# LoRA adapters gated once for both batches, with A and B taken through DRAM

## The chip, the cores and the metric

The kernel runs on one core of one Trainium2 chip. The core has TensorE (PE) for matrix products, VectorE (DVE), ScalarE (ACT) and GpSimd (POOL) for elementwise work, SyncE (SP) as an issuer of DMAs, an on-chip memory of 128 partitions (SBUF), and PSUM, into which TensorE writes. The metric is the device time of one execution in microseconds. The time before is the median of three runs.

## What is computed

x is (2, 1024, 2048), ctx is (2, 2048, 2048), the FFN kernel is 2048 x 2048, all f32. Cut to what matters here:

```python
x = x + matmul(fake_quant(layernorm(x)), fake_quant(ctx))        # cross attention part
z = layernorm(x)
base_out = matmul(z, kernel) + bias                              # FFN
x_flat = z.reshape(8, -1, 2048)                                  # 8 groups of 256 tokens
A_eff = einsum('bn,nri->bri', gate, lora_A)                      # 8 x 32 x 2048, from 16 adapters
B_eff = einsum('bn,nor->bor', gate, lora_B)                      # 8 x 2048 x 32
Ax    = einsum('bri,bti->btr', A_eff, x_flat)
delta = einsum('bor,btr->bto', B_eff, Ax)
Ax_s  = einsum('ri,bti->btr', lora_A_shared, x_flat)             # the shared adapter
delta = delta + einsum('or,btr->bto', lora_B_shared, Ax_s)
out   = x + base_out + delta
```

"Gating" is the making of A_eff and B_eff: a weighted sum over 16 adapters, with one set of 16 weights for each of 8 groups of tokens. Groups 0 to 3 belong to the first batch, 4 to 7 to the second.

## The kernel before

**Tiling.** The two batches are worked through one after the other by the loop at line 672. A batch has 1024 tokens, held in y as four tiles of 256 tokens (g = 0 to 3) by 2048. The 2048 output columns are four blocks of 512 (n = 0 to 3).

**Stages of a batch.** First, x is normalised, quantised and transposed into c1T (prep_x), and the context is quantised one block n at a time into c2[n] (quantise: a loaded slice goes through ScalarE into a q2b buffer, and from there through DVE into bf16). column_term sums a block over the rows on TensorE (tile pc). xattn_pair multiplies (tile pa) one group g by one block n, in two halves j of 16 matmuls; a ScalarE instruction writes the start value of each half into PSUM beforehand (line 340), and DVE adds the result to y and takes statistics. Then y is normalised into z, transposed on TensorE (tile ptz) and copied by ScalarE into the tiles zq, which are also stored to DRAM as zs. lora_ax multiplies z by the gated and shared A (tiles px, axT). Last comes the FFN as seven outer products of seven inner ones (product, line 590; chains fu, fv, fw), with the operands loaded as blocks and combined on DVE and GpSimd. Delta adds the adapters' output in between (tile pl); it reads B from DRAM into bp by a DMA that ScalarE issues (line 454). While the first batch is at its last outer product, the second batch's first context block and x are prepared (meanwhile).

**Gating.** The adapters' A and B lie in DRAM with 512 rows, one for each adapter and rank, in four chunks c of 8 ranks x 16 adapters = 128 rows. A matmul with the matrix gmat (128 rows by 4 groups x 8 ranks = 32 columns) gives one chunk's gated rows. In gated (line 357) the four chunks of one column block write four strips of 32 partitions of one PSUM tile:

```python
row = (2 * h + c) * GP
nc.tensor.matmul(ps[row : row + GP, :], gmat..., t[:, c, :], start=True, stop=True, skip_group_check=True)
```

DVE copies that tile into a q2b buffer (line 376). lora_a_step transposes the four 128-column pieces on TensorE (tile pga) and lets DVE put them into acat, the left operand of lora_ax (line 387). lora_b_step writes the q2b buffer with eight DMAs on SP into the batch's own DRAM tensor bd[b] (line 397). Both are called four times in each batch: A for n = 0, 1 between the quantise steps of block 2 (line 717), A for n = 2, 3 after groups 1 and 2 of block 2 (line 730), B for n = 0 after block 2 (line 733) and for n = 1 to 3 after the groups of block 3 (line 751). gmat is made anew at the top of each batch (line 673).

**What sets the order.** Each engine works through its own list in order. The lists are made at build time by a scheduler that orders instructions by a model of their times, so an instruction can stand between others that come earlier or later in the text; DVE's sums in the FFN are tied in a fixed line. Loads of context and adapters are issued by load_next in the order of the list todo (lines 155 to 165), into the ten buffers lit; SP issues them, the weight loads (line 520), the writes to bd and, in the FFN, the reads of zs. q2b has three buffers, shared by quantise and gated. The PSUM pool ps_m has two buffers, shared by the tiles pt, pc, pg, pga, ptz and px. The pools hand out buffers in turn.

Of the kernel before, what the change touches and what calls it, by code (L numbers as in the profile page):

```python
# [20 lines left out]
P = 128  # L21
# [45 lines left out]
def tile_quant_xattn_then_lora_ffn(  # L67
# [30 lines left out]
    H = D // 2  # L98
    KH = KT // 2
    KQ = KT // 4  # L100
    GP = GPB * RC

    const = ctx.enter_context(tc.tile_pool(name="const", bufs=1))
    small = ctx.enter_context(tc.tile_pool(name="small", bufs=4))
# [15 lines left out]
    bp = Bufs([const.tile([P, NB], F32, tag=f"bp{i}", name=f"bp{i}") for i in range(2)])  # L120
    bias_b = Bufs([const.tile([P, NB], F32, tag=f"bias{i}", name=f"bias{i}") for i in range(1)])
    axT = const.tile([P, GPB // 2, GT], F32, tag="axT", name="axT")
    gmat = const.tile([P, 2, GPB // 2, RC], F32, tag="gmat", name="gmat")
    st1 = const.tile([P, MT, NN, 6], F32, tag="st1", name="st1")
    st2 = const.tile([P, MT, NN, 6], F32, tag="st2", name="st2")
    r_s = const.tile([P, MT], F32, tag="r_s", name="r_s")
# [4 lines left out]
    ]  # L131


    bd = [dram.tile([GPB, 2, R, D], F32, tag=f"bd{b}", name=f"bd{b}") for b in range(B)]

    def bf(t, n):

# [18 lines left out]
    for b in range(B):  # L156
        for n in range(2):
            todo.extend((b, raw_src(b, n, r)) for r in range(KT // 2))
        for n in range(2, 4):
            for r in range(KT // 2):  # L160
                todo.append((b, raw_src(b, n, r)))
                if r in ((3, 7) if n == 2 else (5, 7)):
                    todo.extend((b, ad_src(la, 2 * (n - 2) + r // 6 if n == 3 else r // 4, h)) for h in range(2))
        for n in range(NN):
            todo.extend((b, ad_src(lb, n, h)) for h in range(2))
    loaded = deque()
    ahead = [2]
# [14 lines left out]
    def next_loaded():  # L182
        return loaded.popleft()
# [55 lines left out]
    )  # L239
    gval = const.tile([P, GB], F32, tag="gval", name="gval")  # L240
    nc.vector.tensor_tensor(gate_b, gate_b, m_ad.unsqueeze(1).to_broadcast([P, GB, NL]), ALU.mult)
    for b in range(B):
        for i in range(2):
            nc.vector.tensor_reduce(
                gval[:, ds(b * GPB + i * 2, 2)], gate_b[:, b * GPB + i : (b + 1) * GPB : 2, :], AX.X, ALU.add
            )

    def norm_stats(stats, name):  # L250
# [103 lines left out]
        return summed  # L354


    def gated(nm):

        ps = ps_m.tile([P, NB], F32, tag="pm", name=f"pg_{nm}")
        for h in range(2):  # L360
            buf, t = next_loaded()
            for c in range(2):
                row = (2 * h + c) * GP
                nc.tensor.matmul(  # L364
                    ps[row : row + GP, :],
                    gmat.rearrange("p i a r -> p (i a r)"),
                    t[:, c, :],
                    start=True,
                    stop=True,
                    skip_group_check=True,  # L370
                )
            lit.give(buf)
            load_next()
        st = q2b.take()
        sf = st.rearrange("p k n -> p (k n)").bitcast(F32)
        nc.vector.tensor_copy(sf, ps)
        return st, sf

    def lora_a_step(b, n):

        st, sf = gated(f"a{b}_{n}")
        pt = ps_m.tile([P, KQ, P], F32, tag="pm", name=f"pga_{b}_{n}")
        for k in range(KQ):
            nc.tensor.transpose(pt[:, k, :], sf[:, ds(k * P, P)], ident)
        q2b.give(st)
        for g in range(GPB):
            nc.vector.tensor_copy(
                acat[:, ds(n * KQ, KQ), own_col[g], :].rearrange("p k (c r) -> p k c r", c=NC),
                pt.rearrange("p k (c i a r) -> p i a k c r", c=NC, i=2, r=RC)[:, g % 2, g // 2],
            )  # L390

    def lora_b_step(b, n):

        st, sf = gated(f"b{b}_{n}")
        for c in range(NC):
            for i in range(2):
                nc.sync.dma_start(
                    out=bd[b][i::2, i, ds(c * RC, RC), ds(n * NB, NB)],
                    in_=sf[ds(c * GP + i * (GP // 2), GP // 2), :],
                )  # L400
        q2b.give(st)

    def prep_z(b, m, zq, wk):

# [34 lines left out]
    class Delta:  # L439
# [7 lines left out]
        def step(self):  # L447
            if not self.units:
                return
            pr, n, j = self.units.popleft()  # L450
            cols = ds(n * NB, NB)
            if j == 0:
                self.bp, self.bb = bp.take(), bias_b.take()
                nc.scalar.dma_start(
                    out=self.bp, in_=bd[self.b][ds(2 * pr, 2), :, :, cols].rearrange("g s r n -> (g s r) n")
                )
# [213 lines left out]
            big.give(t)  # L670

    for b in range(B):
        nc.vector.tensor_tensor(
            gmat.rearrange("p i a r -> p (i a) r"),
            m_rk.unsqueeze(1).to_broadcast([P, GPB, RC]),
            gval[:, ds(b * GPB, GPB)].unsqueeze(2).to_broadcast([P, GPB, RC]),
            ALU.mult,
        )
        if b == 0:
            open_c2(0)  # L680
            prep_x(0, 0, c1T, wk)
# [21 lines left out]
        for g in range(2, GPB):  # L703
            for m in range(g * MG, (g + 1) * MG):
                with tc.issue_after(opened.ins):
                    prep_x(b, m, c1T, wk)
            for n in range(2):
                xattn_pair(b, n, g, c1T, c2[n])
                if g + 1 == GPB:
                    close_c2(n)  # L710
                    open_c2(n + 2)
                    bp.give(colt.pop(n))
                    if n == 0:
                        for r in range(NR):
                            quantise(c2[2], r)
                            if r % 4 == 3:
                                lora_a_step(b, r // 4)
                        column_term(b, 2, c2[2])
        if b == 0:
            for pr in range(GPB // 2):  # L720
                nc.sync.dma_start(out=acat[:, :, 3 * pr + 1, :], in_=a_sh)
            for bb in range(B):
                for g in range(GPB):
                    nc.sync.dma_start(out=bd[bb][g, 1 - g % 2], in_=b_sh)
        for g in range(GPB):
            xattn_pair(b, 2, g, c1T, c2[2])
            for r in {0: range(3), 1: range(3, 6), 2: range(6, 8), 3: ()}[g]:
                quantise(c2[3], r)
            if 1 <= g <= 2:
                lora_a_step(b, g + 1)  # L730
            if g == 2:
                column_term(b, 3, c2[3])
        lora_b_step(b, 0)
        close_c2(2)
        bp.give(colt.pop(2))
        first = Operands(b, 0)
# [2 lines left out]
        for g in range(GPB):  # L739
            xattn_pair(b, 3, g, c1T, c2[3])  # L740
            big.give(c1T_bufs[g])
            if g == 0:
                first.block("b11")
                first.load("b12")
            elif g == 1:
                first.block("b12")
                first.comb("t1", "b12", "b11", ALU.subtract)
            elif g == 2:
                first.load("b22")
            if g < 3:  # L750
                lora_b_step(b, g + 1)
            if g > 0:
                zqs[g - 1] = [lit.take() for _ in range(4)]
                group_z(b, g - 1, wk, zqs[g - 1])
            if g == 2:

                lora_ax(b, 0, [zqs[0], zqs[1]])
                for i in range(2):
                    for j in range(2):
                        first.t[f"a{i + 1}{j + 1}"] = zqs[i][j]  # L760
                        lit.give(zqs[i][2 + j])
# [127 lines left out]
```

## Time and profile before

Median of three runs: 1131.94 us (1130.91 to 1132.06).

| What | Value |
|---|---|
| the profiled execution's own time | 1128.31 us |
| its span | 1126.5 us |
| granted TensorE clock | 1.00 |
| q2b<-lit on ScalarE (quantise, line 310) | 64 of 1230 ns |
| pg_a, pg_b on TensorE (line 364) | 64 + 64 records, mean 605 ns |
| pga on TensorE (line 384) | 32 records, mean 274 ns |
| adapter loads on SP (line 179) | 32 + 32 of 256 KB |
| bd<-q2b on SP (line 397) | 64 of 32 KB |
| HBM read, written | 224.99 MB, 37.75 MB |

Times count from the start of the span. "Busy" is time in which an engine executes, "idle before" is the time just before an instruction in which its engine did nothing, with what released it. A matmul of f32 operands makes two records in the profile, one of bf16 operands makes one; successive matmuls overlap, so the start of the next instruction tells more than a record's own duration. By the chain of work that ended last, TensorE carries 81% of the span, DVE 8%, DMA 6% and ScalarE 4%. The first batch's gating runs from 102.9 us (first pg_a) to 189.6 us, the second's from 644.1 to 731.1 us. The FFN of the first batch is in full course from about 242 us, that of the second from about 782 us.

### The profile page before, as it was taken

How to read it: one execution, taken by the hardware profiler on the slowest of the kernel's cores; microseconds unless marked ns; L12 is line 12 of the kernel's file. 1: busy time of each engine (PE TensorE's matmuls, PEld its weight loads, DVE VectorE, ACT ScalarE, POOL GpSimd, SP SyncE). 2: the span in 40 equal slices, each digit the busy share in tenths (PEclk: the TensorE clock that was granted, in tenths of full speed). 3: DMA queues.
4: the chain of work that ended last, by engine and by line, in shares of the span. 5: the costliest groups of instructions: out<-in, count | busy, mean ns of one | idle time of the engine just before them, and what ended most of it. 6: DMA issues, size and time to landing. Idle time of an engine off the chain costs nothing.

```text
span 1126.5 us, 10325 instructions
## 1 busy us (share of the span) xinstructions
PE 1076.9 (96%) x3782; PEld 483.3 (43%) x3782; DVE 734.3 (65%) x961; ACT 261.4 (23%) x342; POOL 263.9 (23%) x105
## 2 busy tenths in 40 slices
PE   1689999999999999999999999999999999999998
PEld 0344435544444444444444444455444444444443
DVE  4675538566595767568766654666668586865861
ACT  4975413210001010001384761232000000000000
POOL 0000000234344422525000000022435343243600
PEclk9999999999999999999999999999999999999999
DMA  8991936886689747489866093688668875649611
GB/s 304 395 245 38 294 109 239 306 304 211 247 281 373 265 172 261 158 304 338 302 204 188 1 268 96 235 328 313 233 219 289 298 254 183 253 146 321 213 38 56
DMA packets 120771, 261.33 MB, mean 232 GB/s; under 512 B 11920, under 2 KB 16144, under 8 KB 119568
## 3 DMA queue, kind: packets, MB, share of 16 engines
q1 hardware_dynamic: 99264, 218.65, 57.0%
q10 hardware_dynamic: 21456, 42.02, 10.8%
q8 instruction: 30, 0.49, 0.2%
q14 instruction: 21, 0.17, 0.0%
HBM read 224.99 MB, written 37.75 MB: 233 GB/s over the span
## 4 chain that ended last, share of the span: by engine, by line
PE 81%; DVE 8%; DMA 6%; ACT 4%; issue 1%; SPq 0%; DVEq 0%; ACTq 0%
PE fu L590 33%; PE fv L590 17%; PE pa L342 13%; PE fw L590 8%; PE pl L462 3%; DVE st L279 2%; PE ptz L413 2%; DMA y<-in_x_dram 2%; PE pc L327 2%; DVE big L539 1%; DMA zs<-lit 1%; DMA bd<-q2b 1%; PE pg_a L364 1%; ACT big L291 1%; PE pg_b L364 1%
## 5 line engine op out<-in xcount | busy, mean ns | idle before, releaser
L590 PE MATMUL fu<-big,lit 128*128 128x512 f32 x896 | 396.3, 594 | 0.6 <-DVE y L608 0.6
L539 POOL TENSOR_TENSOR lit<-lit,lit 128x1024 f32<-128x1024 f32 x56 | 161.9, 2898 | 539.5 <-DMA zs<-lit 207.6
L590 PEld LDWEIGHTS fu<-big,lit 128*128 128x128 f32 x896 | 167.7, 190 | 212.4 <-issue 211.4
L342 PE MATMUL pa<-big,big 128*128 128x512 bf16 x1024 | 234.1, 379 | 8.4 <-ACT pa L340 7.2
L590 PE MATMUL fv<-big,lit 128*128 128x512 f32 x448 | 198.1, 594 | 0.0
L530 POOL TENSOR_TENSOR lit<-lit,lit 128x1024 f32<-128x1024 f32 x40 | 101.6, 2539 | 285.6 <-DMA lit<-zs 253.5
L539 DVE TENSOR_TENSOR big<-big,big 128x2048 f32<-128x2048 f32 x56 | 158.9, 2840 | 5.9 <-PE ptz L413 5.3
L608 DVE TENSOR_TENSOR y<-y,fu 128x1024 f32<-128x1024 f32 (+1 forms) x98 | 113.5, 1193 | 69.5 <-PE fu L590 69.2
L342 PEld LDWEIGHTS <-big 128*128 128x128 bf16 x1024 | 97.5, 98 | 139.1 <-issue 31.9
L590 PEld LDWEIGHTS fv<-big,lit 128*128 128x128 f32 x448 | 84.3, 190 | 108.4 <-issue 108.4
L608 DVE TENSOR_TENSOR y<-y,fv 128x1024 f32<-128x1024 f32 x48 | 56.8, 1218 | 92.5 <-PE fv L590 92.5
L459 ACT COPY pl<-bias 128x1024 f32<-128x1024 f32 x32 | 32.6, 1018 | 346.4 <-DVE y L472 320.9
L310 ACT ACTIVATE q2b<-lit,sc,inv 128x1024 int16<-128x1024 f32 x64 | 76.5, 1230 | 139.6 <-DMA lit<-in_ctx_dram 128.1
L530 DVE TENSOR_TENSOR big<-big,big 128x2048 f32<-128x2048 f32 x40 | 100.7, 2517 | 5.1 <-DMA big<-in_w_dram 5.1
L590 PE MATMUL fw<-big,lit 128*128 128x512 f32 x224 | 100.6, 596 | 0.0
L351 DVE SCALAR_TENSOR_TENSOR y<-pa,k_s,y 128x1024 f32<-128x1024 f32 x32 | 41.0, 1282 | 85.6 <-PE pa L342 85.5
L340 ACT ACTIVATE pa<-bp,r_s 128x512 f32<-128x512 f32 x64 | 42.9, 683 | 98.4 <-DVE y L351 35.4
L590 PEld LDWEIGHTS fw<-big,lit 128*128 128x128 f32 x224 | 41.3, 190 | 52.0 <-issue 50.5
L608 DVE TENSOR_TENSOR y<-y,fw 128x1024 f32<-128x1024 f32 x24 | 28.4, 1215 | 52.7 <-PE fw L590 52.7
L299 PE MATMUL pt<-ident_h,big 128*128 128x128 bf16 x256 | 20.5, 231 | 29.9 <-ACT big L294 29.7
L279 DVE BATCH_NORM_STATS2 st<-y 128x6 f32<-128x512 f32 x64 | 41.7, 675 | 2.7 <-DMA y<-in_x_dram 2.7
L472 DVE TENSOR_TENSOR y<-pl,y 128x512 f32<-128x512 f32 x64 | 41.0, 681 | 1.2
(75 smaller groups left out, 591.2 us busy)
## 6 DMA issues: line engine op xcount, KB each, us to landing
big<-in_w_dram SPq DMA_DIRECT2D x96, 1024.0 KB
lit<-zs SPq DMA_DIRECT2D x88, 512.0 KB
lit<-in_ctx_dram SPq DMA_DIRECT2D x64, 512.0 KB
out_dram<-y ACTq DMA_DIRECT2D x30, 512.0 KB
zs<-lit ACTq DMA_DIRECT2D x24, 512.0 KB
y<-in_x_dram SPq DMA_DIRECT2D x8, 1024.0 KB
lit<-in_lora_a_dram SPq DMA_DIRECT2D x32, 256.0 KB
lit<-in_lora_bt_dram SPq DMA_DIRECT2D x32, 256.0 KB
```

Source lines behind the costliest of these rows:

```text
L279: nc.vector.bn_stats(st1[:, m, n, :], ym[:, ds(n * NB, NB)])
L310: nc.scalar.activation(qi, t, AF.Relu, bias=z2, scale=inv2)
L340: nc.scalar.activation(pa[:, j, :], colt[n], AF.Identity, bias=r_s[:, m : m + 1])
L342: nc.tensor.matmul(pa[:, j, :], c1T[g][:, k, ds(j * P, P)], c2[k // 8][:, k % 8, :], start=False, stop=(k == KT - 1), skip_group_check=True,)
L351: summed = nc.vector.scalar_tensor_tensor(yp, pa, s12, yp, ALU.mult, ALU.add)
L459: nc.scalar.copy(pl, self.bb.unsqueeze(1).to_broadcast([P, 2, NB]))
L462: nc.tensor.matmul(pl[:, i, :], axT[rows, pr, ds(j * P, P)], self.bp[rows, :], start=False, stop=True, skip_group_check=True,)
L472: line(nc.vector.tensor_add(yb, pl[:, i, :], yb))
L530: line(eng.tensor_tensor(got[0], got[0], got[1], ALU.add if terms[1][2] > 0 else ALU.subtract))
L539: line(eng.tensor_tensor(out_t, at[p], at[q], op))
L590: nc.tensor.matmul(ps[:, m, :], at[:, k, ds(m * P, P)], bt[:, k, :], start=(opens and k == 0), stop=(ends and k == KQ - 1), skip_group_che ...
L608: line(nc.vector.tensor_tensor(yp, yp, chains[chain][:, js, :], ALU.add if sign > 0 else ALU.subtract))
```

## The change

gmat gets 64 columns: all eight groups of both batches, made once before the loop. gated is called for one half h (two chunks) at a time: two matmuls that write two strips of 64 partitions, one copy into q2b, and four DMAs on SP into a DRAM tensor. It is called only in the first batch, eight times for A (tensor ad) and eight for B (tensor bd, now one for both batches). A no longer goes from q2b to the transposes: in each batch lora_at_step reads two column blocks of the batch's half of ad back into a lit buffer, twice, and makes the eight transposes and four wider copies into acat. These reads stand after group 1 of block 2 and after group 0 of block 3. The adapter loads of the second batch are taken out of todo.

```diff
-    GP = GPB * RC
+    GP = GB * RC
-    bd = [dram.tile([GPB, 2, R, D], F32, tag=f"bd{b}", name=f"bd{b}") for b in range(B)]
+    ad = dram.tile([2, GB // 2, R, D], F32, tag="ad", name="ad")
+    bd = dram.tile([GB, 2, R, D], F32, tag="bd", name="bd")
...
-                if r in ((3, 7) if n == 2 else (5, 7)):
+                if b == 0 and r in ((3, 7) if n == 2 else (5, 7)):
...
-        for n in range(NN):
+        for n in range(NN if b == 0 else 0):
             todo.extend((b, ad_src(lb, n, h)) for h in range(2))
...
-    def gated(nm):
+    def gated(nm, n, h, dst):
         ps = ps_m.tile([P, NB], F32, tag="pm", name=f"pg_{nm}")
-        for h in range(2):
-            buf, t = next_loaded()
-            for c in range(2):
-                row = (2 * h + c) * GP
-                nc.tensor.matmul(ps[row : row + GP, :], ...)
-            lit.give(buf)
-            load_next()
+        buf, t = next_loaded()
+        for c in range(2):
+            nc.tensor.matmul(ps[c * GP : (c + 1) * GP, :], ...)
+        lit.give(buf)
+        load_next()
         st = q2b.take()
         sf = st.rearrange("p k n -> p (k n)").bitcast(F32)
         nc.vector.tensor_copy(sf, ps)
-        return st, sf
+        for c in range(2):
+            for i in range(2):
+                nc.sync.dma_start(
+                    out=dst[i][:, ds((2 * h + c) * RC, RC), ds(n * NB, NB)],
+                    in_=sf[ds(c * GP + i * (GP // 2), GP // 2), :],
+                )
+        q2b.give(st)
...
+    def lora_a_step(n):
+        for h in range(2):
+            gated(f"a_{n}_{h}", n, h, ad)
+    def lora_b_step(n):
+        own = [bd[i::2, i] for i in range(2)]
+        for h in range(2):
+            gated(f"b_{n}_{h}", n, h, own)
+    def lora_at_step(b, n2):
+        buf = lit.take()
+        t = flat(buf)
+        nc.sync.dma_start(
+            out=t, in_=ad[:, ds(b * GPB // 2, GPB // 2), :, ds(2 * n2 * NB, 2 * NB)].rearrange("i a r n -> i (a r) n")
+        )
+        for n in range(2):
+            pt = ps_m.tile([P, KQ, P], F32, tag="pm", name=f"pga_{b}_{n2}_{n}")
+            for k in range(KQ):
+                nc.tensor.transpose(pt[:, k, :], t[:, ds((n * KQ + k) * P, P)], ident)
+            for pr in range(GPB // 2):
+                nc.vector.tensor_copy(
+                    acat[:, ds((2 * n2 + n) * KQ, KQ), 3 * pr : 3 * pr + 3 : 2, :],
+                    pt.rearrange("p k (i a r) -> p a k i r", i=2, r=R)[:, pr],
+                )
+        lit.give(buf)
...
-                            if r % 4 == 3:
-                                lora_a_step(b, r // 4)
+                            if b == 0 and r % 4 == 3:
+                                lora_a_step(r // 4)
...
-            if 1 <= g <= 2:
-                lora_a_step(b, g + 1)
+            if b == 0 and 1 <= g <= 2:
+                lora_a_step(g + 1)
+            if g == 1:
+                lora_at_step(b, 0)
...
-        lora_b_step(b, 0)
+        if b == 0:
+            lora_b_step(0)
...
-            if g < 3:
-                lora_b_step(b, g + 1)
+            if g == 0:
+                lora_at_step(b, 1)
+            if b == 0 and g < 3:
+                lora_b_step(g + 1)
```

More of the change, by code (lines that the diff above doesn't have):

```diff
@@ L122, in tile_quant_xattn_then_lora_ffn @@
     axT = const.tile([P, GPB // 2, GT], F32, tag="axT", name="axT")
-    gmat = const.tile([P, 2, GPB // 2, RC], F32, tag="gmat", name="gmat")
+    gmat = const.tile([P, 2, GB // 2, RC], F32, tag="gmat", name="gmat")
     st1 = const.tile([P, MT, NN, 6], F32, tag="st1", name="st1")
@@ L241, in tile_quant_xattn_then_lora_ffn @@
     nc.vector.tensor_tensor(gate_b, gate_b, m_ad.unsqueeze(1).to_broadcast([P, GB, NL]), ALU.mult)
[L242 to L246, printed above, removed]
+    for i in range(2):
+        nc.vector.tensor_reduce(gval[:, ds(i * GB // 2, GB // 2)], gate_b[:, i::2, :], AX.X, ALU.add)
+    nc.vector.tensor_tensor(
+        gmat.rearrange("p i a r -> p (i a) r"),
+        m_rk.unsqueeze(1).to_broadcast([P, GB, RC]),
+        gval.unsqueeze(2).to_broadcast([P, GB, RC]),
+        ALU.mult,
+    )
     def norm_stats(stats, name):
@@ L354, in xattn_pair @@
         return summed
-    def gated(nm):
+    def gated(nm, n, h, dst):
         ps = ps_m.tile([P, NB], F32, tag="pm", name=f"pg_{nm}")
-        for h in range(2):
-            buf, t = next_loaded()
-            for c in range(2):
-                row = (2 * h + c) * GP
[L364 to L371, printed above, removed]
-            lit.give(buf)
-            load_next()
+        buf, t = next_loaded()
+        for c in range(2):
+            nc.tensor.matmul(
+                ps[c * GP : (c + 1) * GP, :],
+                gmat.rearrange("p i a r -> p (i a r)"),
+                t[:, c, :],
+                start=True,
+                stop=True,
+                skip_group_check=True,
+            )
+        lit.give(buf)
+        load_next()
         st = q2b.take()
@@ L376, in gated @@
         nc.vector.tensor_copy(sf, ps)
-        return st, sf
[L379 to L395, printed above, removed]
+        for c in range(2):
             for i in range(2):
                 nc.sync.dma_start(
-                    out=bd[b][i::2, i, ds(c * RC, RC), ds(n * NB, NB)],
+                    out=dst[i][:, ds((2 * h + c) * RC, RC), ds(n * NB, NB)],
                     in_=sf[ds(c * GP + i * (GP // 2), GP // 2), :],
@@ L401, in lora_b_step @@
         q2b.give(st)
+    def lora_a_step(n):
[19 more added lines that the diff above has]
+                    pt.rearrange("p k (i a r) -> p a k i r", i=2, r=R)[:, pr],
+                )
+        lit.give(buf)
     def prep_z(b, m, zq, wk):
@@ L454, in step @@
                 nc.scalar.dma_start(
-                    out=self.bp, in_=bd[self.b][ds(2 * pr, 2), :, :, cols].rearrange("g s r n -> (g s r) n")
+                    out=self.bp, in_=bd[ds(self.b * GPB + 2 * pr, 2), :, :, cols].rearrange("g s r n -> (g s r) n")
                 )
@@ L672, in tile_quant_xattn_then_lora_ffn @@
     for b in range(B):
[L673 to L678, printed above, removed]
         if b == 0:
@@ L721, in tile_quant_xattn_then_lora_ffn @@
                 nc.sync.dma_start(out=acat[:, :, 3 * pr + 1, :], in_=a_sh)
-            for bb in range(B):
-                for g in range(GPB):
-                    nc.sync.dma_start(out=bd[bb][g, 1 - g % 2], in_=b_sh)
+            for g in range(GB):
+                nc.sync.dma_start(out=bd[g, 1 - g % 2], in_=b_sh)
         for g in range(GPB):
```

## The prediction

> **What bounds the kernel now.** I read the engine totals first, then the slices, then TensorE's waits, then its timeline where the adapters are gated.
>
> ```profile
> PE 1076.9 (96%) x3782; PEld 483.3 (43%) x3782; DVE 734.3 (65%) x961; ACT 261.4 (23%) x342; POOL 263.9 (23%) x105
> ```
>
> ```profile
> PE   1689999999999999999999999999999999999998
> ```
>
> The first line is the engine totals, the second TensorE's busy tenths in 40 slices. TensorE (PE) is busy for 96% of 1126.5 us, and the idle part lies in the first three slices. From about 90 us on only TensorE's own work, or a new wait of it, can move the end. Its waits say the same of the two stretches that the change touches, 95 to 245 us in the first batch and 560 to 785 us in the second: the longest single wait there is 1.1 us.
>
> How gating looks on TensorE (columns: start, duration, instruction, tiles, records):
>
> ```profile
> 132.27 1.05 PE L364 MATMUL pg_a<-lit,gmat 128*32 128x512 f32 x2
> 133.25 3.63 PE L342 MATMUL pa<-big,big 128*128 128x512 bf16 x16
> 136.80 1.06 PE L364 MATMUL pg_a<-lit,gmat 128*32 128x512 f32 x6
> 137.79 2.33 PE L342 MATMUL pa<-big,big 128*128 128x512 bf16 x10
> ...
> 188.61 1.07 PE L364 MATMUL pg_b<-lit,gmat 128*32 128x512 f32 x8
> 189.61 2.98 PE L342 MATMUL pa<-big,big 128*128 128x512 bf16 x13
> ```
>
> One f32 matmul makes two records. The reader is to see that one matmul (x2), three (x6) and four (x8) take the same time from start to the next line: 0.98, 0.99, 1.00 us. The four write different 32-column strips and run at once; a group costs about 0.98 us whatever its size. So what counts is groups. Of the 16 calls of gated, 10 are split by the scheduler (x2, then x6 later) and 6 are whole: 26 groups, 13 in each batch, 12.8 us per batch.
>
> **Second batch: what goes.** All 13 groups go: 12.8 us. The 0.4 us that pga waited there for DVE's copy goes too. The 16 transposes stay (lora_at_step makes the same number), so they change nothing. The loads removed (32 of 256 KB, 8.4 MB) and 32 writes to bd lay beside TensorE's work and are worth nothing themselves; they free SP's queue ahead of the context loads and the weight loads. What is late next? The column sum pc_2 needs eight quantised slices at 1.23 us of ScalarE each, 9.8 us after the first column block's buffer comes free, and TensorE now has some 3 us less to do in that time; I give back 0.6 us. The two reads of ad stand before the weight loads on SP, long after ad was written. Second batch: -13.2 + 0.6 = **-12.6 us**.
>
> **First batch: TensorE's own work.** A 64-column tile leaves room for two matmuls at once. The nearest row is lora_ax, whose pairs of 64-column tiles do run so (its group, with busy us, mean ns and idle before it; then its piece in the chain of work that ended last, with start and us):
>
> ```profile
> L429 PE MATMUL px<-lit,acat 128*64 128x256 f32 x192 | 28.5, 381 | 0.0
> ```
>
> ```profile
> 741.73 7.06 PE px L429 x64
> ```
>
> These are 32 matmuls in 7.06 us, so 16 pairs at 0.44 us for 256 columns; for 512 columns 0.86 us, and about 0.98 with the change of tiling. In the built programs' order the first batch issues, for A: 1 matmul, later 1+2; 2; 2; 1, later 1+2; 2+2; for B: 2+2; 2+2+2; 2; 2+2. A lone group is 0.98 us, each further step behind it 0.86 (in "1+2" the first runs beside one of the two). A: 2.82 + 1.96 + 2.82 + 1.84; B: 1.84 + 2.70 + 0.98 + 1.84; sum 16.8 us against 12.8 now: **+4.0 us**.
>
> Here a rule speaks against the change. The Trainium skill, TensorEngine Tiling (Array Packing), Theoretical Speedup, gives up to 4x for 32 columns and up to 2x for 64. By it the 16 calls need 16 packs of four before and 8 x 2 packs of two after: no TensorE time saved. By the row it is 26 groups before and 16.8 us after, because the scheduler had cut 10 packs in two. The same page (Key Properties) says that a change of tiling mode drains TensorE; the row's 0.98 against 0.86 puts that at 0.12 us. I take the rows: 25.6 - 16.8 = 8.8 us of TensorE work saved in all.
>
> **First batch: new waits.** Each half now goes PSUM, DVE copy, q2b, four writes on SP, DRAM. The rows (two groups as before, then one tile's writes with least, median and longest issue in ns):
>
> ```profile
> L376 DVE COPY q2b<-pg_a 128x512 f32<-128x512 f32 x8 | 5.4, 681 | 0.0
> L387 DVE COPY acat<-pga 128x128 f32<-128x128 f32 x32 | 7.1, 283 | 5.0 <-PE pga L384 5.0
> ```
>
> ```profile
> L397 SPq DMA_DIRECT2D bd<-q2b x64: 567/567/831, 156.7 to 741.2; - x64
> ```
>
> SP issues four writes in 2.3 us; then they must land. No row shows an ad write. The chain of waits has two bd writes:
>
> ```profile
> 187.25 8.71 DMA zs<-lit
> 195.98 5.46 DMA bd<-q2b
> 201.46 7.32 DMA bd<-q2b
> ```
>
> 5.5 and 7.3 us, but behind two weight loads and zs stores. The low end is the about 2 us of the Trainium skill's DMA: Bandwidth & Descriptors (the fixed cost, mostly the wait for the write's receipt). Ahead of the first ad writes only two context loads (1 MB) stand in the queue, so I take 3 us and keep 7.3 for the range. A q2b buffer is then away 0.7 + 2.3 + 3 = 6 us, and there are three for quantise and gating.
>
> I laid the new order against the old clock (DVE, ScalarE and SP each in order):
> - Behind the first two q2b copies on DVE stand two statistics (1.3 us), and behind them the quantise steps; ScalarE quantises with one q2b buffer until the ad writes land. The start value of pa_1_3's second half is queued behind that on ScalarE, at 115.7 us; TensorE wants it at 114.8: 0.9 us. Slices 7 and 8 of pc_2 get their buffers when ad lands, about 115 and 117.5 us; pc_2 reads them near 121: nothing, with 3 us of cover.
> - pc_2 now stands behind most of pa_1_3, so pa_2_0 waits for pc_2's DVE and ScalarE steps: 0.5 us.
> - Before the second pair of A columns, the four acat copies (256 elements, between the 0.28 us of 128 and the 0.68 of 512: estimate 0.41) stand behind y's update, and ps_m has two buffers: gating waits 1.4 us, pc_3 0.4.
> - The first read of ad is issued near 146 us and due about 154.5; the second near 173, behind a weight load, due about 183: both covered, by 3 to 4 us.
> - Behind pga_1 the same again on ps_m, with weight sums of 2.3 and 2.8 us between the q2b copies on DVE: 1.4 us, and 0.7 for the first z transposes, which need the same two PSUM buffers.
>
> Sum 5.3 us, less 0.6 us of waits that the old order had in this stretch (pga 0.42, pa 0.22): **+4.7**. ScalarE's bp reads still wait for the bd writes of their columns, now near 204 us instead of 208.8; TensorE lost only 0.8 us by that and I leave it. Added SP work is 32 ad writes (18 us of issue over 70 us in which SP is mostly waiting), 4 reads of 512 KB and half as many, twice as large, bd writes. Behind a waiting ad write stand context loads for the fourth block, whose pc_3 has over 20 us of cover, and B loads, which have as much. The one gmat of 64 columns and two wider reductions lie in the first 40 us, where TensorE waits for x and context; cost nothing.
>
> **Sum.** -12.6 + 4.0 + 4.7 = -3.9 us. Against the profiled execution's own 1128.31 us (span 1126.5) that is 1124.4. That execution is 3.6 us below the median of the timed runs, 1131.94; the same step from the median gives **1128.0 us**.
>
> **Rivals.**
> 1. *Landing takes the place of the gating* (slower). If ad and bd writes take the 7.3 us of the contended row, a q2b is away 10 us. Then pc_2's last slices come about 3 us late, the n=1 writes hold ScalarE, with the start values behind them, for some 2 us, and DVE stalls at the q2b copies before y's update and z: 3.5 us. +8.5 on the sum: +4.6, **1136.5 us**. It decides from about 6 us of landing on, where the 3 us of cover ends. For it: that row, and one ring that carries ctx, w, ad and bd. Against: DMA share is 0.36 at 90 to 120 us.
> 2. *The first batch stays dense*: the new waits fall on work that can slide; only +4.0 is left: -12.6 + 4.0 = -8.6, about **1123.3 us**. For it: no TensorE wait now is over 1.1 us. Against: four new places where two PSUM buffers and an ordered DVE meet.
> 3. *Waits just eat the gain*: landing of 4 to 6 us or one read of ad late by 2 to 4 us: **1131 us**, no change.
> 4. *The change doesn't pack*: the two matmuls run in turn. 32 x 0.86 + drains, about 28 us instead of 16.8: +7.3, **1139**. px speaks against it.
>
> **Chances.** Forecast 0.45, rival 1 0.27, rival 2 0.13, rival 3 0.12, rival 4 0.03. A measurement of this kernel tells 0.2%, 2.3 us, from no change. The forecast's own range is 1125 to 1130.5; most of it (0.38) is faster by that bound, the rest even. Faster 0.50, same 0.19, slower 0.31. The 8-in-10 range reaches from rival 2 to rival 1: 1123 to 1137.
>
> **What would show it.** Right: no gating records after 250 us; the stretch that was 644 to 770 us is about 12.6 us shorter; its TensorE stays without waits over 1 us; first FFN starts 8 to 9 us later; pg records in the first batch 64. Wrong: ScalarE or DVE waiting on "DMA ad" or "DMA bd" for several us, TensorE waiting for pc, pa or pga (rival 1); pga waiting for lit from ad; paired pg records one after the other (rival 4). The forecast falls if first-batch waits come to over 9 us or under 2.

## The result and the profile after

The changed kernel takes **1167.26 us** (median of 4 runs, 1165.11 to 1172.17), the kernel before 1131.97. The ratio is 1.032 (95% interval 1.0298 to 1.034): it is slower by 3.2%, where 0.3% less had been forecast. Its profiled span is 1165.8 us.

The page of the changed kernel, engine totals first, then TensorE's slices and its granted clock in tenths:

```profile
PE 1082.5 (93%) x3718; PEld 491.3 (42%) x3718; DVE 738.5 (63%) x942; ACT 261.8 (22%) x342; POOL 263.3 (23%) x105
...
PE   1689976969999999999999999989999999999998
...
PEclk6899988979999999999999999989999999999999
```

64 matmul records are gone, as the diff says, and TensorE is still busy for longer (1082.5 us against 1076.9). The row of slices has dents in the sixth, seventh and ninth slice, between 146 and 262 us, where there was none; beside them the clock falls to 8, 8 and 7 tenths. (The 6 and 8 at the head of the clock row lie in the start, ahead of the first `pa`, which comes 0.6 us later than before.) TensorE's waits (us in total, times, longest):

```profile
PE pga L407 <- DMA lit<-ad: 16.5, 2, 8.9
PE ptz L425 <- DVE big L421: 14.1, 4, 7.2
PE pa L345 <- ACT pa L343: 9.8, 11, 1.7
```

The first is new, and the second came to 0.5 us before. The transposes of the gated A rows wait 16.5 us for the two reads of `ad` in the first batch, and the z transposes wait 14.1 us for DVE's z. TensorE's timeline (start, duration, instruction, tiles, records, in brackets the idle time before and its cause):

```profile
111.39 1.08 PE L365 MATMUL pg_a<-lit,gmat 128*64 128x512 f32 x4
...
134.77 1.07 PE L365 MATMUL pg_a<-lit,gmat 128*64 128x512 f32 x2
135.77 3.63 PE L345 MATMUL pa<-big,big 128*128 128x512 bf16 x16
139.33 1.93 PE L365 MATMUL pg_a<-lit,gmat 128*64 128x512 f32 x6
141.19 9.10 PE L345 MATMUL pa<-big,big 128*128 128x512 bf16 x41
...
163.79 1.94 PE L407 MATMUL pga<-ident,lit 128*128 128x128 f32 x8 [7.59 <-DMA lit<-ad]
165.77 3.01 PE L365 MATMUL pg_a<-lit,gmat 128*64 128x512 f32 x8
...
201.88 1.97 PE L407 MATMUL pga<-ident,lit 128*128 128x128 f32 x8 [8.95 <-DMA lit<-ad]
...
253.37 1.94 PE L425 MATMUL ptz<-ident,big 128*128 128x128 f32 x8 [7.18 <-DVE big L421]
```

The first five lines are the gating as forecast: a pair (x4) takes 1.01 us to the start of the next instruction (112.40), a lone matmul (x2) 1.00 us, and three in a row ("1+2", x6, the first beside one of the two others) 1.86 us. The lines with brackets are waits. Behind each wait eight transposes take 1.94 us, where eight take 1.04 without one (in e1_split_read, below); the windows behind the first wait, and two behind the last, show why (us, length, then busy time and count for each engine, the granted clock, the share of the 16 DMA engines, GB/s):

```profile
158.00:160.00 2.00, 0.00 (x0) 0.00 (x0) 0.00 (x0) 0.00 (x0) 0.00 (x0) 1.00 0.13 53
160.00:162.00 2.00, 0.00 (x0) 0.00 (x0) 0.00 (x0) 0.00 (x0) 0.00 (x0) 0.79 0.13 53
162.00:164.00 2.00, 0.21 (x1) 0.24 (x2) 0.00 (x0) 0.00 (x0) 0.00 (x0) 0.50 0.13 50
...
166.00:168.00 2.00, 2.00 (x6) 0.59 (x6) 1.33 (x4) 0.00 (x0) 0.00 (x0) 0.51 0.74 204
168.00:170.00 2.00, 2.00 (x10) 0.60 (x7) 1.64 (x3) 0.00 (x0) 0.00 (x0) 1.00 0.85 265
...
260.00:262.00 2.00, 2.00 (x3) 0.50 (x2) 0.07 (x1) 0.00 (x0) 0.00 (x0) 0.50 0.97 379
...
264.00:270.00 6.00, 6.00 (x23) 3.21 (x22) 1.30 (x2) 1.91 (x4) 0.00 (x0) 1.00 0.02 8
```

Two things are to be seen. While the read of `ad` is the only transfer, the DMA share is 0.13: two engines of 16, at 50 GB/s. In the trace the first read is 128 recorded packets of 4096 bytes, 172 ns each on average, spread over 11.1 us: two at a time. And the clock is halved 5.0 us into this idle time (2.4 and 3.7 us into the two others) and comes back only 4.2 us after work resumes (3.6 us after the second wait, 10.2 us after the one that ends at 253.37).

**Where the time went.** I cut TensorE's timeline at three marks: the first matmul of the FFN's `fv` chain in either batch, and the first `pa` of the second batch. From the first mark to that `pa` (345.4 us) and from the second `fv` to TensorE's last instruction (333.6) all kernels below agree within 0.1 us; the start, up to the first `pa`, takes 41.3 to 42.5. So nearly everything happens in two stretches, from the first `pa` to the first `fv` of each batch; lengths in us, added up from the profiled executions:

| kernel | first batch | of it idle | pg | all else | second batch |
|---|---|---|---|---|---|
| before | 206.4 | 9.6 | 12.8 | 184.0 | 194.4 |
| changed | 247.6 | 36.0 | 18.7 | 192.9 | 191.9 |
| e1_split_read | 234.2 | 24.9 | 18.5 | 190.8 | 191.0 |
| before_one (control) | 207.7 | 10.7 | 13.8 | 183.2 | 196.9 |
| split_one | 219.4 | 17.1 | 19.0 | 183.3 | 185.8 |

The first batch got 41.2 us longer, the second only 2.5 us shorter. Of the 41.2, idle is 26.4, gating 5.9, and 8.9 is that the same work took longer, which is about what the half clock makes: 4.2, 3.6 and 10.2 us of work behind the three waits, at half speed, or 9 us lost. (Of the first batch's 512 `pa` records 13 are missing in e1_split_read and 15 in before_one and split_one, 0.22 us each, so up to 2.9 and 3.3 us of their idle time is work.)

The profiled execution of the kernel before ran 3.6 us under its median. So the change costs 39.3 us by the spans and 35.3 by the medians. The profiled executions of before_one and before_short lie within 0.7 us of their medians and have 196.9 and 195.7 us in the second batch; against these the second batch's gain is 3.8 to 5.0 us rather than 2.5.

### The profile page after: what moved, and what is told of

Its sections match the earlier page's. It is cut to its first block, busy times and chain, and to the rows that moved or that the text cites. A ratio compares the mean times of both kernels' runs of the same rounds, so it can differ in the third digit from the quotient of the medians.

```text
span 1165.8 us, 10132 instructions
## 1 busy us (share of the span) xinstructions
PE 1082.5 (93%) x3718; PEld 491.3 (42%) x3718; DVE 738.5 (63%) x942; ACT 261.8 (22%) x342; POOL 263.3 (23%) x105
## 4 chain that ended last, share of the span: by engine, by line
PE 76%; DVE 9%; DMA 8%; ACT 4%; issue 2%; SPq 1%; DVEq 0%; ACTq 0%
PE fu L602 32%; PE fv L602 16%; PE pa L345 10%; PE fw L602 8%; DMA big<-in_w_dram 4%; PE pl L474 3%; DMA lit<-ad 3%; PE pc L330 2%; PE ptz L425 2%; DVE st L282 2%; ACT big L294 1%; DVE big L551 1%; ACT big L297 1%; DMA lit<-in_ctx_dram 1%; DVE big L421 1%
## 5 line engine op out<-in xcount | busy, mean ns | idle before, releaser
L425 PE MATMUL ptz<-ident,big 128*128 128x128 f32 x256 | 38.4, 294 | 15.2 <-DVE big L421 14.1
L421 DVE TENSOR_SCALAR big<-y,mv_z,rstd_z 128x1024 f32<-128x1024 f32 x32 | 30.4, 972 | 31.1 <-PE ptz L425 31.0
```

What stands on the lines that cost most here:

```text
L421: nc.vector.tensor_scalar(t, y[g][:, m % MG, ds(h * H, H)], mean, rstd, ALU.subtract, ALU.mult)
L425: nc.tensor.transpose(pt[:, k, :], t[:, ds((4 * u + k) * P, P)], ident)
```

## The experiments

**e1_split_read: the read of ad in two halves.**

```diff
-        nc.sync.dma_start(
-            out=t, in_=ad[:, ds(b * GPB // 2, GPB // 2), :, ds(2 * n2 * NB, 2 * NB)].rearrange("i a r n -> i (a r) n")
-        )
+        for i in range(2):
+            nc.sync.dma_start(
+                out=t[ds(i * P // 2, P // 2)],
+                in_=ad[i, ds(b * GPB // 2, GPB // 2), :, ds(2 * n2 * NB, 2 * NB)].rearrange("a r n -> (a r) n"),
+            )
```

> Changed kernel, but each read of ad is two DMAs of 64 rows (source dimensions 64 x 1024) in place of one whose source starts with a dimension of 2. Same place in SP's list. Theory T (the read runs on two of the 16 DMA engines, because its outermost source dimension is 2): it lands in under 6 us instead of 14.7 and 19.1, TensorE's 16.5 us of waits on lit<-ad go to under 2, the slow TensorE stretches behind them (4 us) go as well, total 1141 to 1150 us. Rival Q (the read is late because B loads and weight loads stand before it in SP's queue): nothing changes in landing, total 1162 to 1170 us.

Measured: 1151.79 us, ratio 1.0175 (1.016 to 1.019), a little over the expected range. The waits for `ad` are gone; the same 512 KB, issued at 148.2 us, is transposed at 155.10 where it had been 163.79. One spell of half clock, 3.4 us at 159.4, is left in this place. So it was the shape of the read, not the landing of the writes or the queue ahead of it. The Trainium skill, DMA: Bandwidth & Descriptors, section "Why a DMA increments its semaphore by 16 and not by 1", says that a transfer runs on the largest number of engines up to 16 that divides the slowest dimension of both of its access patterns; the source `i (a r) n` has 2 there, each half has 64. The 0.13 of the windows agrees. 20 us over the kernel before remain. Their largest piece in the chain of work that ended last of this kernel (start, us, what):

```profile
208.91 0.26 PE ptz L427 x3
209.17 12.24 DMA big<-in_w_dram
...
221.47 0.58 SPq L380
...
224.23 12.14 DMA big<-in_w_dram
...
236.39 0.04 DVE big L544
...
239.56 2.83 DVE big L423
...
242.53 1.94 PE ptz L427 x8
```

DVE's sums of the weight operands keep one order, b11, b12, b22, b21, and this sum is the fourth. So the two loads are those of b21. They follow one another on SP, at 209.17 and 224.23 us, with writes to `bd` (L380) between them, of which one waits 6.9 us for the first load; each load takes 12 us, and only then can DVE sum them (L544) and go on to z (L423). In the kernel before the same loads were issued at 203.53 and 208.46 us (SP and DVE; x3 counts the load behind them too):

```profile
203.53 16.29 SPq L520 DMA_DIRECT2D big<-in_w_dram  x3
216.63 2.79 DVE L530 TENSOR_TENSOR big<-big,big 128x2048 f32<-128x2048 f32 x1 [1.09 <-DMA big<-in_w_dram]
```

The sum of b21 is 20 us late. Two of the expectations below call these loads b22's; what they say of 185 and 189 us in the kernel before is b22's time, not b21's.

**left_out: the kernel before without the second batch's gating** (its second batch uses the first batch's gated A and B).

```diff
-                if r in ((3, 7) if n == 2 else (5, 7)):
+                if b == 0 and r in ((3, 7) if n == 2 else (5, 7)):
...
-        for n in range(NN):
+        for n in range(NN if b == 0 else 0):
...
-            if 1 <= g <= 2:
+            if b == 0 and 1 <= g <= 2:
                 lora_a_step(b, g + 1)
...
```

> Kernel before, with the second batch's gating left out (loads of A and B, pg, pga, writes to bd; the second batch uses the first batch's acat and bd). The first batch is as before. Theory of the prediction: -12.6 us, and 1.8 us more for 16 transposes that also go, about 1117 to 1119 us. Theory W (the second batch's weight loads, released by pa and waited for by DVE, become the bound when the gating between them goes): 1124 to 1130 us, with DVE waiting 5 us or more on big<-in_w and TensorE on DVE behind it.

Measured: 1123.89 us, ratio 0.9931 (0.9916 to 0.9946), just under theory W's range; in the second batch 188.8 us instead of 194.4. Of TensorE's work 14.7 us are gone there (12.8 of gating, 1.9 of transposes), and not even this pure removal brings that: by the profiles it brings 5.6 us in the stretch, by the timed runs 8.0. The chain of this kernel:

```profile
718.61 0.66 PE pa L342 x3
719.29 8.54 DMA big<-in_w_dram
...
727.92 2.29 DVE big L530
...
730.34 1.18 DVE y L351
...
733.16 0.73 DVE big L409
...
734.03 1.06 PE ptz L413 x8
```

Read it downwards: a `pa` group ends and frees a buffer, only then a weight load is issued, 8.54 us later DVE sums, and z, which DVE has behind that sum, comes late for TensorE. In the kernel before, with gating between them, TensorE's last `pa` of the batch begins at 749.6 us, so that it has work while these loads land; here the last `pa` begins at 725.9. The changed kernel's second batch has the same chain:

```profile
760.82 9.93 DMA big<-in_w_dram
...
770.77 2.29 DVE big L542
...
773.90 0.73 DVE big L421
...
774.77 1.94 PE ptz L425 x8
```

I call it the weight chain; the next runs cut it at different places.

**e1_order: the weight sums of b11 and b22 later in DVE's order** (in the split-read kernel).

```diff
...
-                first.block("b11")
+                with tc.issue_after(summed.ins):
+                    first.block("b11")
...
-        first.block("b22")
+        with tc.issue_after(last_z[0].ins):
+            first.block("b22")
```

> As e1_split_read, and two weight sums on DVE are put later in its list: b11's behind y's update of group 0 of block 3, b22's behind the last z of group 2. Theory W': it is the place of these sums in DVE's list that turns a late weight load into a TensorE wait; 5 to 9 us less than e1_split_read. Rival: the loads are late for TensorE's own use of the sums too, and the wait only moves; within 2 us of e1_split_read.

Measured: 1153.03 us, ratio 1.0182 (1.0165 to 1.0199). No gain. Behind b22's sum b21's moved as well, from 236.39 to 252.29 us, and TensorE now waited for the sum itself, in `fw`:

```profile
PE fw L605 <- DVE big L545: 10.4, 2, 6.6
```

Putting z ahead moved the wait to TensorE's own use of the operand. (The profiled execution is the slowest of the five, 1158.38 us.)

**e1_other_queue: the writes to ad and bd on GpSimd's queue** (in the split-read kernel).

```diff
         for c in range(2):
             for i in range(2):
-                nc.sync.dma_start(
+                nc.gpsimd.dma_start(
                     out=dst[i][:, ds((2 * h + c) * RC, RC), ds(n * NB, NB)],
```

> The split-read kernel (1151.8) with the 64 writes of the gated rows (ad and bd) issued by GpSimd instead of SyncE. Nothing of the computation changes. Theory S: SyncE's order is what made the first batch's b22 loads late (issued at 209 and 224 us instead of 185 and 189, because eight bd writes stood between them, each waiting for an earlier DMA). Then the loads are issued before 200 us, the 6.2 us wait of the z transposes for DVE's weight sum is gone, and the time is 1136 to 1144. Rival B: the loads are issued when pa releases their buffers and no earlier, whatever the queue; then less than 3 us is gained, 1149 to 1153. Rival G: GpSimd issues these writes so slowly that gating waits; then 1152 or more, with TensorE or DVE waiting for q2b.

Measured: 1145.26 us, ratio 1.011 (1.0082 to 1.0138): 6.5 us less than the split read, between theory S (1136 to 1144) and rival B. But theory S's mechanism isn't there. The first batch's weight loads, when they were issued, when DVE's sum began, and when TensorE's last `pa` began (us):

| kernel | b22 issued | b22 summed | b21 issued | b21 summed | last `pa` |
|---|---|---|---|---|---|
| before | 185.30, 188.71 | 200.24 | 203.53, 208.46 | 216.63 | 208.0 |
| changed | 217.83, 218.93 | 233.38 | 235.40, 238.74 | 249.44 | 227.2 |
| e1_split_read | 189.74, 193.26 | 200.41 | 209.17, 224.23 | 236.39 | 202.0 |
| e1_other_queue | 192.91, 206.70 | 215.06 | 217.38, 231.19 | 236.38 | 230.8 |
| split_short (below) | 197.62, 198.17 | 208.91 | 212.77, 214.25 | 227.95 | 221.9 |

Against the split read no load comes sooner: b22's sum is 15 us later, and b21's begins at the same time. What changed is TensorE's own list. The scheduler left `pa` work until 230.8 us, so TensorE has something to do while b21's loads land, and the wait of 6.2 us for z is gone. Two waits of TensorE in this kernel's first batch:

```profile
PE pc L330 <- DVE q2b L377: 5.2, 1, 5.2
PE ptz L427 <- DVE nt_z L265: 2.6, 1, 2.6
```

The first is new: `pc` waits for quantised slices, which wait for a q2b buffer. That is the prediction's q2b step, at 5.2 us once GpSimd issues the writes. Theory G thus holds for one place.

**before_short, left_out_short, split_short: weight loads of half size**, in the kernel before, in left_out and in the split-read kernel. The first FFN step's loads bring 512 KB instead of 1 MB; the other half of each is left out.

```diff
-                    nc.sync.dma_start(out=t, in_=w[ds(k0, KQ * P), ds(n0, NB)].rearrange("(k p) n -> p k n", p=P))
+                    kk = KQ // 2 if self.o == 0 else KQ
+                    nc.sync.dma_start(
+                        out=t[:, :kk, :], in_=w[ds(k0, kk * P), ds(n0, NB)].rearrange("(k p) n -> p k n", p=P)
+                    )
```

> The kernel before, in which the weight loads of the first FFN step of each batch (b11, b12, b22, b21) bring only half of their rows, 512 KB instead of 1 MB; the rest of the tile keeps old data, so that part of the first FFN products is left out as data, while TensorE's and DVE's instructions stay. It is the control for the next two. Theory W says that TensorE's gating covers these loads in the kernel before, so they end nothing: 1128 to 1132. Rival: they already end something: under 1127.

> The second batch's gating left out (1123.9, of which the 13 groups should have given 1119 or less), and with it the same half weight loads as in the control. Theory W: without gating the weight loads end last in the second batch; halved, they land some 3 to 5 us sooner, and the rest of the gating's 12.8 us shows: 1115 to 1120, 11 to 15 us under the control. Rival: it is something else that ends last there (ScalarE's start values, the order of DVE); then the halved loads change nothing: 1122 to 1125.

> The split-read kernel (1151.8) with the same half weight loads as in the control. Theory W: the second batch gains 5 to 8 us, and the first some 6 us, since its b22 loads took 12 us each, one behind the other: 1137 to 1143. Theory S (the queue's order is what counts, not the size): the first batch gains under 3 us and the second 5 to 8: 1142 to 1147. Rival: weight loads are not what the excess of the split-read kernel comes from: 1149 to 1153.

Measured: 1131.08 (ratio 0.9986, 0.9979 to 0.9993), 1126.76 (0.9951, 0.9933 to 0.9969) and 1136.81 us (1.004, 1.003 to 1.005). The control is as the theory has it. split_short gained 15.0 us, the whole of it and more in the first batch (217.0 us from 234.2; second 190.4 from 191.0). That is just below theory W's range in its total, and refutes its split: the gain lies in the first batch, where two 12 us loads had followed one another. Since the last `pa` moved as well, from 202.0 to 221.9 us, size and order are not told apart. left_out_short refutes W outright: no gain. The halved loads still took 3.6 to 6.6 us (5.0 to 8.5 in left_out), TensorE's waits for z came to 8.7 us in three places, and DVE's sums still stood ahead of z. So size alone is not the weight chain's limit in the second batch; the sums belong to it.

**before_one, left_out_one, split_one: one load and no sum for each weight operand of the first FFN step**, in the same three kernels. The second term of each operand is left out.

```diff
-                for K, J, _ in b_terms:
+                for K, J, _ in b_terms[: 1 if self.o == 0 else 2]:
                     t = big.take()
```

> The kernel before, in which each of the four weight operands of the first FFN step of both batches (b11, b12, b22, b21) is one load of 1 MB instead of two loads and DVE's sum of 2.3 us: the second term of each is left out, so part of the data of the first FFN products too, and TensorE's instructions stay. It is the control for the next two. Theory C (the chain from the end of a pa group over its load and DVE's sum to the z transposes is hidden in the kernel before by gating): 1128 to 1132. Rival: it is not hidden: under 1127.

> The second batch's gating left out, and with it the same single loads without sums as in the control. The halved loads gave nothing here (1126.8): they still took 4.8 to 6.6 us to land, and DVE's sum still stood ahead of z in DVE's order. Theory C: with the sums and second loads away, z waits for nothing but pa, and the full 12 to 13 us show: 9 to 14 us under the control, 1115 to 1121. Rival: something else of that stage fills the gap (z's own steps of DVE and ScalarE): 4 to 8 us under the control.

> The split-read kernel (1151.8) with the same single loads without sums as in the control. If theory C is the whole of its excess, what is left is the prediction's own sum (12.6 less in the second batch, 4 to 6 us of TensorE work and some 5 us of small waits more in the first): 1124 to 1131, 0 to 4 us under the control. If the first batch has more waits of its own (q2b, pc, ScalarE's bp), 1132 to 1140.

Measured: 1132.34 us (ratio 0.9999, 0.9988 to 1.001), 1121.30 (0.99, 0.9885 to 0.9915) and 1134.29 (1.0017, 1.0007 to 1.0027). With gating in place, taking the chain out gives nothing: it was hidden. Without gating, the same edit brings left_out to 11.0 us under its control, within theory C's 9 to 14. That is only 2.6 us less than left_out itself, and 3.7 of the 14.7 us still don't come out: TensorE waits 7.2 us for z in four places, where it had waited 5.3 in left_out. And the split-read kernel falls from 1151.8 to 1134.3, 2.0 us over its control: in its second batch 11.1 us shorter than the control, in the first 11.7 us longer, of which gating is 5.2 and idle 6.4; that is the second of the two ranges expected. So cutting the weight chain took away 17.5 us of the 20 that the split read had left, while the control did not move. The edit takes the second loads, the sums and their places in the queues away together, and the scheduler again built another list (last `pa` of the first batch at 221.6 us), so it shows that the excess hangs on these operands and the order built around them, not on which part of the chain.

**whole_packs and whole_packs_axt: the kernel before with its packs of four kept together.** The scheduler had cut ten of sixteen; here gating is issued behind the last `pa` matmul. The second kernel also copies `px` to `axT` on DVE.

```diff
-                nc.tensor.matmul(
+                last_pa[0] = nc.tensor.matmul(
                     pa[:, j, :],
...
-                nc.tensor.matmul(
-                    ps[row : row + GP, :],
+                with tc.issue_after(last_pa[0].ins):
+                    nc.tensor.matmul(
+                        ps[row : row + GP, :],
...
-        nc.scalar.copy(axT[:, pr, :], px)
+        nc.vector.tensor_copy(axT[:, pr, :], px)
```

> Kernel before, with the four gating matmuls of a call held until the preceding pa matmuls are through, so that none of the 16 packs of four is cut in two. Theory of groups (0.98 us each, whatever the size): 10 groups fewer, -9.8 us, about 1122 us. If weight loads take the place in part (theory W): 1125 to 1129 us. If the groups cost by their number of matmuls: no change, 1132 us.

> The kernel whole_packs (1129.8) with the copy of px to axT made by DVE instead of ScalarE; there the copy stood behind the start value of pl, and TensorE's z transposes waited 5.2 us for it in two places. If that wait was on the path: 1124 to 1128. If DVE only takes the place of ScalarE in it: 1129 to 1131. Slower than 1132 if DVE's order makes it later.

Measured: 1129.83 us (ratio 0.9979, 0.9966 to 0.9992) and **1125.79 us** (0.9942, 0.9927 to 0.9957). The groups of whole_packs, with busy us, mean ns and idle before:

```profile
L366 PE MATMUL pg_b<-lit,gmat 128*32 128x512 f32 x64 | 8.5, 605 | 0.0
L366 PE MATMUL pg_a<-lit,gmat 128*32 128x512 f32 x64 | 8.5, 605 | 0.0
```

17.0 us where the kernel before had 27.5. Yet only some 2 us of these 10.5 reach the end. Its waits show two takers:

```profile
PE pa L343 <- ACT pa L341: 9.5, 10, 1.8
...
PE ptz L415 <- ACT axT L439: 5.2, 2, 2.7
```

With the copy on DVE the second is gone, and others have grown (whole_packs_axt):

```profile
PE pa L343 <- ACT pa L341: 12.2, 11, 2.5
PE ptz L415 <- ACT lit L416: 3.3, 4, 2.0
```

By the timed runs this kernel beats both, by 0.6% and 3.6% (1125.79 over 1167.26). Its one profiled execution doesn't show the gain: its span is 1126.5 us, as that of the kernel before; but it was the slowest of this kernel's six, and that of the kernel before lay below its median. I take the timed runs, and don't claim to know where the 0.6% sits.

## Why the prediction was wrong

- **"The first read of ad is issued near 146 us and due about 154.5; the second near 173 ... both covered, by 3 to 4 us": failed.** Issue was at 148.97 and 182.72, but landing took 14.7 and 19.1 us, because each read ran on two engines of 16. I had priced the landing from the number of bytes and never looked at the shape of the transfer. It cost 16.5 us of waits and the half clock behind them, on 7.8 us of work; the split read took back 15.5 us. "pga waiting for lit from ad" stood in the list of what would show the prediction wrong, and that is how it showed.
- **"Second batch: -12.6 us": failed as a sum, not as a count.** What was counted did go (no gating record after 250 us), but the answer to "What is late next?" was wrong. I looked at `pc` (0.6 us) and said of the weight loads only that SP is freed ahead of them. Next in line was the weight chain, which gating had covered: instead of 12.6 us 2.5 came out by the profiles, 3.8 to 5.0 against the controls. With the chain cut, 11.1 us come out.
- **"Added SP work is 32 ad writes ... over 70 us in which SP is mostly waiting": failed.** The list of what stands behind the waiting writes named context and B loads and left out the weight loads. In the changed kernel those of b22 and b21 were issued 30 to 33 us later than before; in the split-read kernel b22's 4 to 5 us and b21's 6 and 16 us later, and b21's sum began 20 us later. Halving these loads took back 15 us. The other queue took back 6.5, but with no load issued earlier, so how much SP's order costs isn't shown.
- **Not in the sum at all: the clock.** Each of three idle times of 7 to 9 us made the work behind it run at half clock for 3.6 to 10.2 us, some 9 us lost in sum in the first batch. The Trainium skill's page TensorE: Matmul & The Clock Gate, Part 1, states both halves of it, a halved clock after an idle window of about 3.4 us and full speed only after as long a busy one; here the clock fell 2.4 to 5.0 us into the idle times, and the last return took about three such windows.
- **"+4.0 us" of TensorE work and "+4.7" of waits in the first batch: right in kind, low by 1 to 2 us each.** With the two other causes cut away (split_one against its control) gating measured 5.2 and idle 6.4.
- **Right: groups, and pairs.** A group of the kernel before cost 0.98 us whatever its size, so whole packs saved 10.5 us of TensorE's gating. 64-column pairs did run at once (1.01 us a pair), so rival 4 fell.
- **Landing of 3 us: right at first, then too low.** The first eight `ad` writes landed in 3.0 to 4.2 us, the others in 4.5 to 7.2, as rivals 3 and 1 had it. Rival 1's sign, ScalarE and DVE waiting on the `ad` writes, was there in the changed kernel:

```profile
ACT q2b L313 <- DMA ad<-q2b: 6.9, 3, 3.9
DVE q2b L377 <- DMA ad<-q2b: 3.7, 1, 3.7
```

It can't have made most of the loss, since ScalarE's stays in split_one (8.1 us), which is 2.0 us over its control. What these waits cost TensorE isn't shown. Rival 1's direction, slower, was right, for a reason that it did not name.

What stays open: how the remaining 11.7 us of the first batch in split_one divide among q2b, PSUM buffers and ScalarE, and how much of the weight chain's cost is the loads, SP's order, DVE's sums or the place of the `pa` work in TensorE's list; the edits that helped moved that place as well.

## What to carry to other kernels

Before a stretch of TensorE work is taken out, follow the chain that runs beside it in the same stretch (buffer freed, load issued, landing, DVE's sum, use): what it lacks in slack is what you will not gain, and an experiment that only leaves the work out prices this before the change is built. For every new transfer read the outermost dimension of both sides as well as the bytes; a reshaped 512 KB read with 2 there took 15 to 19 us. And a new wait of TensorE can cost more than its length: the three of 7 to 9 us here cost some 9 us more, because the clock had to come back.

## What the hardware showed

- 512 KB in 4 KB packets on two DMA engines: 50 GB/s. As two transfers with 64 rows outermost it was no longer waited for.
- The granted clock fell to 0.50 2.4 to 5.0 us into an idle time of 7 to 9 us and came back 3.6 to 10.2 us after work began; eight f32 transposes took 1.94 us instead of 1.04.
- Halving a weight load from 1 MB to 512 KB shortened its landing from 5.0 to 8.5 us (left_out) only to 3.6 to 6.6 us (left_out_short), for the eight loads of the second batch's first FFN step.
- DVE instructions on one column took 1.7 to 2.3 us while GpSimd summed. In left_out_one, DVE's timeline and then GpSimd's:

```profile
738.56 0.15 DVE L259 RECIPROCAL r_z<-sd_z 128x1 f32<-128x1 f32 x1
738.67 0.15 DVE L263 TENSOR_SCALAR nt_z<-nt_z 128x1 f32<-128x1 f32 x1
738.75 2.31 DVE L262 SCALAR_TENSOR_TENSOR nt_z<-ve_z,r_z 128x1 f32<-128x1 f32 x1
740.98 0.15 DVE L265 TENSOR_TENSOR rstd_z<-r_z,nt_z 128x1 f32<-128x1 f32 x1
...
741.28 2.07 DVE L265 TENSOR_TENSOR rstd_z<-r_z,nt_z 128x1 f32<-128x1 f32 x1
```

```profile
735.85 7.49 POOL L539 TENSOR_TENSOR lit<-lit,lit 128x1024 f32<-128x1024 f32 x3 [184.42 <-DMA zs<-lit]
```

The Trainium skill, SBUF — State Buffer, section "SBUF: two separate sides", says that a DVE instruction with two SBUF inputs and a GpSimd one exclude each other for their whole length. The rows agree: L262 and L265, with two tensors in, take 2.31 and 2.07 us, L259 and L263, with one, 0.15. GpSimd's three sums end at 738.62, 741.04 and 743.34 us, and the long DVE instructions at 738.64, 741.06 and 743.35; the L265 that starts between two sums takes 0.15. That adds some 5.5 us ahead of z in this chain (1.70, 2.31 and 2.07 for three instructions that take 0.15 to 0.25 undisturbed), which no sum of mine had held. No run took GpSimd's sums away, so what they cost TensorE isn't shown.
